# Another division of the PSUM banks at the end of the first FFN and in the second FFN

## The chip, the cores and the metric

The kernel runs on one core of one Trainium2 chip. The metric is device time in microseconds (us); the change is judged by its median over several runs. A profiled execution gives the trace: for each engine, what ran when and what it had waited for. Engines: PE (TensorE, matrix multiply; PEld is its weight load), DVE (VectorE), ACT (ScalarE), POOL (GpSimd), SP (which issues the DMAs). Matrix products land in PSUM, which this kernel divides into eight banks of 128 partitions by 512 fp32 values. Results leave a bank through DVE or ACT.

## The reference

Input `x` has 4 sequences of 1024 tokens with 128 features. Three layers with residuals follow one another:

```
x = x + 0.5 * ffn(layernorm(x))
x = x + attn(layernorm(x))          # which normalises once more, and adds its own input
x = x + 0.5 * ffn(layernorm(x))     # the same weights as the first

ffn:  weights = routing(x @ Wr)                 # 8 experts, dense: every expert is computed
      h_e = silu(x @ Wg[e]) * (x @ Wu[e])       # 128 -> 128
      out = sum_e weights[:, e] * (h_e @ Wd[e])
attn: 16 heads of 64, latents of 64 for queries and for keys and values, rotary positions,
      softmax(q k^T / 8) v, output projection
```

## The kernel before, in words

**Blocks.** Tokens are worked in 8 blocks of 512 (`blk`), each through 8 experts (`e`), so an FFN has 64 steps, `n = 8 blk + e`. Each engine works through its own instructions in the order in which the program lists them, which is written out by hand. An instruction that waits holds up those behind it on its engine.

**Banks.** `psA` is two banks (`ps_a` in the trace), `psS[0]` to `psS[3]` are one each (`ps_s`), then `psC` and `psX`. `aux()` (lines 101 to 104) hands out the banks of the list `self.rest` in turn; transposes and other small products use it. A new writer of a bank waits until the last reader of its former content is done; the trace shows this also for readers of other columns of the bank.

**First FFN** (`ffn`, line 364). A step multiplies gate and up (L400) into two of `psS[0..2]`, applies silu on ACT (L402) and the product on DVE (L408). Three steps later `down` (L365 to L372) multiplies by `Wd` into `psC` or `psX`; in the step after that, `gather` scales the result by the routing weights. In blocks 4, 6 and 7 ACT does that (L383, four instructions) and POOL adds it to `X` (L384). In the last 15 steps `self.rest` holds `psX` and `psS[3]` (L829), since the first attention work uses them, and all downs go to `psC`. The last three downs (experts 5, 6, 7 of block 7) have no other step of the FFN between them.

**Attention.** Scores (L703), exponentials (L707), sums on POOL (L719), values (L726), a pass that finds row maxima (L675, L676), and the making of rotated queries and keys for later heads in between (L593 to L615): products into two banks (L593), four products with tables on DVE (L581), a rounding on ACT (L607), a remainder on POOL (L612), and two DMAs out; the latents for it (C_l) are loaded by a DMA on SP (L586 through the helper at L47). Scores of odd slots use `psS[2]` and `psS[3]`.

**Second FFN** (`ffn2`, line 415). The gate and up products of a step (L479) take two of `psS[0]`, `psS[1]`, `psS[2]`, `psC`. ACT applies silu (L482), DVE multiplies twice (L492 with the up product, L493 with the routing weight), ACT rounds (L486), POOL forms the remainder (L487). Three steps later `down` (L434) adds three products to the sum of the block, over all 8 experts, in one bank: `psS[3]` for even blocks, `psX` for odd ones (L432). Four steps after the block's last step ACT copies the sum out (L447), one step later PE transposes it (L453) and DVE adds it to `X` (L455), which SP writes out. The last block does this in two halves.

Beside it, in the first steps, the last two attention outputs are projected (L771) and added (L773), and `ffn_pre` prepares blocks 6 and 7: norm (L227), transposes (L256), two copies on DVE (L258, L259), router logits (L269), read by DVE (L270), then the routing (L290 to L348) and a transpose of the weights (L357). All of these products take their bank from `aux()`, whose list holds one bank here, the first of `psA` (L960).

Of the kernel before, what the change touches and what calls it, by code (L numbers as in the profile page):

```python
# [17 lines left out]
B, S, D = 4, 1024, 128  # L18
H, DH = 16, 64
E = 8  # L20
# [17 lines left out]
class Kernel:  # L38
# [325 lines left out]
    def ffn(self, hp, tp, xs_of, wts, bg, depth, acts):  # L364
        nc, X = self.nc, self.X  # L365
        hs, gathers = [], []

        def down(blk, e, hT):
            pd = self.psX if e % 2 and self.psX not in self.rest else self.psC
            for i in range(4):  # L370
                nc.tensor.matmul(pd[:, i * 128:(i + 1) * 128], hT[:, i * 128:(i + 1) * 128], self.wd[:, e, :], start=True, stop=True)  # L371
            gathers.append((blk, e, pd))  # L372

        def gather(blk, e, pd):
            t = blk * 4
            assert blk in self.routed, (blk, e, len(self.routed))
            if e % 4 == 0 and blk not in acts:
                for i in range(4):
                    nc.vector.scalar_tensor_tensor(X[:, t + i, :], pd[:, i * 128:(i + 1) * 128], wts[:, t + i, e:e + 1], X[:, t + i, :], ALU.mult, ALU.add)
            else:  # L380
                tmp = tp.tile([128, 4, 128], F32, name="dtmp", tag=f"t{e % 3}")
                for i in range(4):
                    nc.scalar.activation(tmp[:, i, :], pd[:, i * 128:(i + 1) * 128], AF.Identity, scale=wts[:, t + i, e:e + 1])  # L383
                nc.gpsimd.tensor_tensor(X[:, t:t + 4, :], X[:, t:t + 4, :], tmp, ALU.add)  # L384
            if e == E - 1:
                self.done.add(blk)

        for n in range(2 * B * E + depth + 1):
            if gathers:
                gather(*gathers.pop(0))  # L390
            sh = None
            if n < 2 * B * E:
                blk, e = divmod(n, E)
                xs = xs_of(blk)
                assert blk in self.ready
                bg(n, 0)
                ps = [self.psS[(2 * n + k) % 3] for k in range(2)]
                for w, p in zip((self.wg, self.wu), ps):
                    for k, (a, c) in enumerate(((0, 0), (0, 1), (1, 0))):
                        nc.tensor.matmul(p, w[:, a, e, :], xs[:, c, :], start=k == 0, stop=k == 2)  # L400
                sh = hp.tile([128, 2, 512], F32, name="p")
                nc.scalar.activation(sh[:, 0, :], ps[0], AF.Silu)  # L402
                bg(n, 1)
            if len(hs) == depth or (hs and sh is None):
                down(*hs.pop(0))
            if sh is not None:
                bg(n, 2)
                nc.vector.tensor_tensor(sh[:, 1, :], sh[:, 0, :], ps[1], ALU.mult)  # L408
                bg(n, 3)
                hs.append((blk, e, sh[:, 1, :]))  # L410
        for g in gathers:
            gather(*g)


    def ffn2(self, xs_of, bg, out):
        nc, X = self.nc, self.X
        N, DEPTH, LEAD, NB = 2 * B * E, 3, 4, 4
        nbank = 0
        hs, later, wbs, split = [], {}, [], []

        def weights(n):
            blk, e = divmod(n, E)
            assert blk in self.routed, blk
            wb = self.prep.tile([128, 512], F32, name="wb", tag=("t0", "t1", "t2", "t3", "hi_r")[n % 5])
            h = blk % 2
            nc.sync.dma_start(out=wb, in_=self.wt_scr[blk // 2][e:e + 1, 512 * h:512 * h + 512].to_broadcast([128, 512]))
            wbs.append(wb)

        def down(n, sh):
            blk, e = divmod(n, E)  # L430
            if e == 0:
                self.po = (self.psS[3], self.psX)[blk % 2]  # L432
            for k, (a, c) in enumerate(((0, 0), (1, 0), (0, 1))):
                nc.tensor.matmul(self.po, self.wd[:, a, e, :], sh[:, c].bitcast(F32R), start=e == 0 and k == 0, stop=e == E - 1 and k == 2)  # L434
            if e == E - 1:
                finish(n, blk, self.po)

        def finish(n, blk, po):
            o = self.prep.tile([128, 512], F32, name="fo", tag="xs2")
            last = blk == NT // 4 - 1  # L440
            t = blk * 4
            parts = [slice(0, 2), slice(2, 4)] if last else [slice(0, 4)]

            def copy():
                for p in parts:
                    c = slice(128 * p.start, 128 * p.stop)
                    nc.scalar.copy(o[:, c], po[:, c])  # L447

            def turn():
                for p in parts:  # L450
                    pt = self.aux()
                    for i in range(p.start, p.stop):
                        nc.tensor.transpose(pt[:, i * 128:(i + 1) * 128], o[:, i * 128:(i + 1) * 128], self.ident)  # L453
                    xs = X[:, t + p.start:t + p.stop, :]
                    nc.vector.tensor_tensor(xs, xs, pt.rearrange("p (t d) -> p t d", t=4)[:, p], ALU.add)  # L455
                    nc.sync.dma_start(out=out[:, t + p.start:t + p.stop, :], in_=xs)

            for k, fn in enumerate((copy, turn)):
                if last:
                    fn()  # L460
                else:
                    later.setdefault(n + DEPTH + 1 + k, []).append(fn)

        for n in range(LEAD):
            weights(n)
        for n in range(N + DEPTH):
            for fn in later.pop(n, ()):
                fn()
            if n < N:
                blk, e = divmod(n, E)  # L470
                xs = xs_of(blk)
                assert blk in self.ready
                ps = []
                for _ in range(2):
                    ps.append(self.psS[nbank % NB] if nbank % NB < 3 else self.psC)
                    nbank += 1
                for w, p in zip((self.wg, self.wu), ps):
                    for k, (a, c) in enumerate(((0, 0), (0, 1), (1, 0))):
                        nc.tensor.matmul(p, w[:, a, e, :], xs[:, c, :], start=k == 0, stop=k == 2)  # L479
                gh = self.op1.tile([128, 2, 512], F32, name="ptmp") if n % 3 == 2 else self.prep.tile([128, 2, 512], F32, name="eo", bufs=2)  # L480
                g, h = gh[:, 0, :], gh[:, 1, :]
                nc.scalar.activation(g, ps[0], AF.Silu)  # L482
            if split:
                m, hp = split.pop()
                sh = self.pp.tile([128, 2, 512], F32R, name="p")
                nc.scalar.copy(sh[:, 0, :], hp)  # L486
                (nc.gpsimd if m < N - 1 else nc.vector).tensor_tensor(sh[:, 1, :], hp, self.f(sh[:, 0, :]), ALU.subtract)  # L487
                hs.append((m, sh))
            if hs and hs[0][0] == n - DEPTH:
                down(*hs.pop(0))  # L490
            if n < N:
                nc.vector.tensor_tensor(h, g, ps[1], ALU.mult)  # L492
                nc.vector.tensor_tensor(h, h, wbs.pop(0), ALU.mult)  # L493
                split.append((n, h))
                if n + LEAD < N:
                    weights(n + LEAD)
                bg(n)
# [279 lines left out]
    def run(self):  # L777
# [88 lines left out]
        a, c, e = (NP - 3) % 3, (NP - 2) % 3, (NP - 1) % 3  # L866
# [90 lines left out]
        with ExitStack() as ctx:  # L957
            self.ready, self.routed = set(range(6)), set(range(6))
            assert not (streams[1] or streams[2])
            self.rest, self.bankO = [self.psA[:, 0, :]], None  # L960
            last = [self.accp.tile([128, 2, 512], F32R, name="acc") for _ in range(2)]
            x_of = lambda blk: last[blk - 6] if blk >= 6 else xs[blk // 2][:, :, 512 * (blk % 2):512 * (blk % 2) + 512]
            g = self.ffn_pre(self.prep, (6, 7), x_of, self.wts2[:, 3].rearrange("p e t -> p t e"), rows=3)

            def bg2(n):
                self.run_later(NGRP + 1 + n)
                if n >= GS:
                    next(g, 0)
                if n >= GD:
                    next(g, 0)  # L970

            self.ffn2(x_of, bg2, self.out.rearrange("(n p) d -> p n d", p=128))
# [55 lines left out]
```

## Time and profile before

| | us |
|---|---|
| median of 3 runs | 1803.73 (1801.5 to 1804.94) |
| the profiled execution's own time | 1803.11 |
| its span, first to last instruction | 1801.3 |
| PE busy | 1726.3 (96%) |
| DVE busy | 1339.9 (74%) |
| POOL busy | 1339.3 (74%) |
| ACT busy | 908.9 (50%) |
| 234.5 to 242.4: PE busy, of 7.9 | 5.24 |
| 1699.0 to 1706.0: PE busy, of 7.0 | 1.80 |
| 1637 to 1802: all waits of PE | 13.0 |

The shares of the page are means over the whole span; what a wait is worth depends on the stage. The first FFN ends and attention begins near 242, and the second FFN runs from 1637.6 to the end. PE is shown with the clock that it was granted, 1.00 being full speed; the mean over the span is 0.989. In a timeline line the first number is the start, the second the duration, then come engine, line, operation, output <- inputs and a count; brackets hold the idle time before it and what ended it. A down projection of four matmuls shows as x8, since each runs as two passes.

### The profile page before, as it was taken

What the parts mean: (1) busy time and instruction counts of PE and PEld (TensorE: products, weight loads), DVE (VectorE), ACT (ScalarE), POOL (GpSimd) and SP (SyncE); (2) the same over time, 40 slices, a digit from 0 to 9 for tenths busy, and PEclk for the clock granted to TensorE, in tenths of its full rate; (3) what the DMA queues carried; (4) which work ended last, traced back from release to release, by engine and by line L of the source; (5) the groups of instructions that cost most, each with busy time, mean ns of one, the idle gap of its engine ahead of it and who ended that gap; (6) DMA issues with size and microseconds to landing.
All of it is one profiled execution on the core that took longest, in us unless ns stands there. A gap on an engine that the chain in (4) does not pass through costs nothing.

```text
span 1801.3 us, 31304 instructions
## 1 busy us (share of the span) xinstructions
PE 1726.3 (96%) x11492; PEld 1030.3 (57%) x11492; DVE 1339.9 (74%) x1903; ACT 908.9 (50%) x1916; POOL 1339.3 (74%) x803
## 2 busy tenths in 40 slices
PE   7988889999999999999999999999999999999898
PEld 5777655555555555555555555555555555556676
DVE  6776658877777778777688777788777776835787
ACT  4666555444545445554444445454444444445454
POOL 4458678778887788877788777788888765556566
PEclk9999989999999999999999999999999999999899
DMA  6025445444444444454444544454444432124443
GB/s 196 1 71 170 135 129 165 145 145 147 130 142 142 150 145 130 130 153 142 141 135 136 160 140 131 143 142 147 136 144 140 130 95 72 31 96 129 129 124 100
DMA packets 129674, 232.80 MB, mean 129 GB/s; under 512 B 36336, under 2 KB 49776, under 8 KB 128880
## 3 DMA queue, kind: packets, MB, share of 16 engines
q1 hardware_dynamic: 129520, 230.80, 42.7%
q8 instruction: 90, 1.47, 0.4%
q14 instruction: 64, 0.52, 0.1%
HBM read 146.45 MB, written 84.02 MB: 128 GB/s over the span
## 4 chain that ended last, share of the span: by engine, by line
PE 78%; DVE 7%; ACT 7%; POOL 3%; issue 3%; DMA 1%; SPq 1%; ACTq 0%; POOLq 0%; DVEq 0%
PE psc L726 24%; PE ps_s L703 21%; PE ps_a L675 8%; PE ps_s L738 5%; ACT p L707 4%; PE psx L771 4%; PE ps_s L400 3%; PE ps_s L479 3%; PE psx L593 2%; DVE m L676 2%; PE psc L371 1%; PE psc L479 1%; PE psx L434 1%; PE ps_s L434 1%; ACT dtmp L383 1%
## 5 line engine op out<-in xcount | busy, mean ns | idle before, releaser
L676 DVE TENSOR_REDUCE m<-ps_a 128x2 f32<-128x1024 f32 x512 | 627.3, 1225 | 324.1 <-PE ps_a L675 323.9
L707 ACT ACTIVATE p<-ps_s 128x512 f32<-128x512 f32 x1024 | 531.0, 601 | 605.6 <-PE ps_s L703 605.4
L719 POOL TENSOR_TENSOR acc<-acc,p 128x1024 f32<-128x1024 f32 x256 | 609.7, 2382 | 43.0 <-ACT p L707 31.6
L726 PE MATMUL psc<-p,ckn 128*64 128x512 f32 x2048 | 496.2, 605 | 0.0
L703 PE MATMUL ps_s<-QT,KT 64*128 64x512 f32 x3072 | 447.3, 393 | 0.1
L719 POOL TENSOR_TENSOR acc<-p 128x1024 f32<-128x1024 f32 x64 | 152.2, 2377 | 251.4 <-ACT p L707 251.3
L703 PEld LDWEIGHTS ps_s<-QT,KT 64*128 64x128 f32 x3072 | 296.7, 185 | 60.2 <-issue 3.2
L726 PEld LDWEIGHTS psc<-p,ckn 128*64 128x64 f32 x2048 | 124.3, 136 | 213.7 <-issue 199.4
L675 PE MATMUL ps_a<-KT,QT 64*128 64x512 f32 x1024 | 234.6, 450 | 11.2 <-DVE m L676 11.0
L675 PEld LDWEIGHTS ps_a<-KT,QT 64*128 64x128 f32 x1024 | 98.5, 184 | 229.9 <-issue 83.8
L703 PE MATMUL ps_s<-maxr,one_row 64*128 64x512 f32 x1024 | 210.0, 392 | 1.0 <-DMA maxr<-mr 1.0
L612 POOL TENSOR_TENSOR eo<-eo,hi_r 128x512 fp32r<-128x512 f32 x128 | 185.0, 1463 | 0.0
L766 DVE TENSOR_TENSOR osb<-osb,rB 128x512 f32<-128x512 f32 x64 | 153.8, 2403 | 3.0 <-DMA rB<-d 3.0
L384 POOL TENSOR_TENSOR X<-X,dtmp 128x512 f32<-128x512 f32 x54 | 69.0, 1278 | 73.2 <-ACT dtmp L383 66.7
L703 PEld LDWEIGHTS ps_s<-maxr,one_row 64*128 64x128 f32 x1024 | 103.4, 185 | 23.0 <-DMA maxr<-mr 2.2
L487 POOL TENSOR_TENSOR p<-eo,p 128x512 fp32r<-128x512 f32 x42 | 62.6, 1496 | 42.0 <-ACT p L486 35.5
L602 POOL TENSOR_TENSOR eo<-rt,rt 128x512 f32<-128x512 f32 x64 | 81.8, 1279 | 0.0
L600 POOL TENSOR_TENSOR eo<-rt,rt 128x512 f32<-128x512 f32 x64 | 81.8, 1278 | 0.0
L607 ACT CAST hi_r<-eo 128x512 fp32r<-128x512 f32 x128 | 74.6, 640 | 6.9 <-DMA qs<-hi_r 3.6
L400 PE MATMUL ps_s<-xs,wg 128*128 128x512 f32 x192 | 66.6, 457 | 11.8 <-DVE p L408 10.7
L728 ACT COPY osb<-psc 128x512 f32<-128x512 f32 x64 | 37.6, 588 | 72.8 <-PE psc L726 72.8
L771 PEld LDWEIGHTS psx<-G,osb 128*128 128x128 f32 x496 | 60.8, 193 | 21.2 <-issue 21.2
(194 smaller groups left out, 2131.8 us busy)
## 6 DMA issues: line engine op xcount, KB each, us to landing
C_l<-cs SPq DMA_DIRECT2D x64, 512.0 KB
QT<-qs SPq DMA_DIRECT2D x256, 128.0 KB
KT<-ks SPq DMA_DIRECT2D x256, 128.0 KB
qs<-hi_r SPq DMA_DIRECT2D x32, 512.0 KB
qs<-eo SPq DMA_DIRECT2D x32, 512.0 KB
ks<-hi_r SPq DMA_DIRECT2D x32, 512.0 KB
ks<-eo SPq DMA_DIRECT2D x32, 512.0 KB
rB<-d SPq DMA_DIRECT2D x128, 128.0 KB
```

Source lines behind the costliest of these rows:

```text
L400: nc.tensor.matmul(p, w[:, a, e, :], xs[:, c, :], start=k == 0, stop=k == 2)
L600: nc.gpsimd.tensor_tensor(w["eo"][:, 0, :], w[0, 0], w[1, 1], ALU.subtract)
L612: nc.gpsimd.tensor_tensor(eo.bitcast(F32R), eo, self.f(w["hi"][:, int(stage[2]), :]), ALU.subtract)
L675: nc.tensor.matmul(self.psA[:, hh, :], self.QT[P % 3][r, 0, q0:q0 + 128], self.KT[P % 3][r, 0, kk * 512:kk * 512 + 512], start=True, stop= ...
L676: nc.vector.tensor_reduce(self.m_of[U][:, :, qb, kk], self.psA, AX.X, ALU.max)
L703: nc.tensor.matmul(ps, w, x, start=k == 0, stop=k == 3)
L707: nc.scalar.activation(self.p_of[s][:, hh, :], ps, AF.Exp, scale=0.125)
L719: nc.gpsimd.tensor_tensor(acc, self.p_of[s - 1] if c == 1 else acc, self.p_of[s], ALU.add)
L726: nc.tensor.matmul(self.psC[64 * hh:64 * hh + 64, :], self.ckn[b % 2][:, c, :], self.p_of[s][:, hh, :], start=c == 0, stop=c == 7)
L738: nc.tensor.matmul(pd[32 * n:32 * n + 32, 0:256], self.ones, part[:, n // 2, 256 * (n % 2):256 * (n % 2) + 256], start=k == 0, stop=k == D ...
L766: nc.vector.tensor_tensor(osb, osb, rB, ALU.mult)
L771: nc.tensor.matmul(po[:, i * 128:(i + 1) * 128], osb[:, i * 128:(i + 1) * 128], self.G[:, j, :], start=True, stop=True)
```

## The change

Three edits. The downs of experts 6 and 7 of the last block of the first FFN go to `psX` and `psS[3]`. The sums of the second FFN all go to `psX`. The list of `aux()` during the second FFN gets `psS[3]` as its second bank, so that the products that use it alternate between two banks. No instruction is added to the work or taken from it, and the order on each engine stays as it was.

```diff
         def down(blk, e, hT):
             pd = self.psX if e % 2 and self.psX not in self.rest else self.psC
+            if blk == 2 * B - 1 and e >= E - 2:
+                pd = (self.psX, self.psS[3])[e % 2]
             for i in range(4):
...
         def down(n, sh):
             blk, e = divmod(n, E)
             if e == 0:
-                self.po = (self.psS[3], self.psX)[blk % 2]
+                self.po = self.psX
...
-            self.rest, self.bankO = [self.psA[:, 0, :]], None
+            self.rest, self.bankO = [self.psA[:, 0, :], self.psS[3]], None
```

## The prediction

> **What bounds the kernel now.** I read the page's shares first (TensorE, PE, is busy 96% of the span; the chain that ended last is 78% PE), then asked for the waits of PE over the two stages that the change touches, and then their timelines. Where PE is the bound, a PE wait counts one for one unless another engine is as late. The attention stage between them (some 250 to 1637 us) is not edited; it can only start earlier.
>
> First place, the end of the first FFN. Columns: start, duration, engine, line, what it does, count, and in brackets the idle time before it and who ended it.
>
> ```profile
> 234.58 1.16 PE L371 MATMUL psc<-wd,p 128*128 128x128 f32 x8 [2.26 <-ACT dtmp L383]
> 235.84 1.14 ACT L383 ACTIVATE dtmp<-psc,wts 128x128 f32<-128x128 f32 x4 [1.31 <-PE psc L371]
> 237.03 2.07 PE L371 MATMUL psc<-wd,p 128*128 128x128 f32 x8 [1.29 <-ACT dtmp L383]
> ...
> 239.20 1.14 ACT L383 ACTIVATE dtmp<-psc,wts 128x128 f32<-128x128 f32 x4 [2.22 <-PE psc L371]
> 240.40 2.07 PE L371 MATMUL psc<-wd,p 128*128 128x128 f32 x8 [1.29 <-ACT dtmp L383]
> ...
> 242.57 1.14 ACT L383 ACTIVATE dtmp<-psc,wts 128x128 f32<-128x128 f32 x4 [2.22 <-PE psc L371]
> ...
> 243.85 1.27 POOL L384 TENSOR_TENSOR X<-X,dtmp 128x512 f32<-128x512 f32 x1 [2.10 <-ACT dtmp L383]
> ...
> 245.09 2.51 POOL L612 TENSOR_TENSOR eo<-eo,hi_r 128x512 fp32r<-128x512 f32 x2
> ...
> 248.05 0.46 SPq L47 DMA_DIRECT2D C_l<-cs  x1
> ```
>
> Three down projections (experts 5, 6, 7 of the last block) share one bank, so PE and ACT take turns. The last addition on POOL follows, then POOL's L612, and behind it on the SP queue the load of C_l, for which PE waits at 252.39 (1.69 us idle). That chain is the bound here, not PE.
>
> Second place, the second FFN:
>
> ```profile
> 1699.95 1.65 ACT L227 ACTIVATE yf<-X,rstdf 128x128 f32<-128x128 f32 x4 [2.18 <-DVE rstdf L222]
> ...
> 1702.49 0.58 ACT L447 COPY fo<-ps_s 128x512 f32<-128x512 f32 x1
> ...
> 1704.40 0.21 DVE L270 TENSOR_REDUCE z<-ps_a 128x32 f32<-128x64 f32 x1
> ...
> 1704.76 1.08 PE L256 MATMUL ps_a<-ident,yf 128*128 128x128 f32 x4 [5.20 <-DVE z L270]
> ...
> 1705.49 1.63 PE L479 MATMUL ps_s<-QT,QT 128*128 128x512 f32 x3
> ```
>
> The transposes of block 7 (L256) have their input at 1701.60 but share a bank with the router logits of block 6, which DVE reads at 1704.40. Of 13.0 us that PE waits from 1637 to 1802, this one is 5.2. From 1740 to 1790 PE is busy 50.00 of 50.00 us.
>
> **Part 1, banks for the last downs.** Only experts 6 and 7 of block 7 move; expert 5 still starts at 234.58, since it waits for ACT after the exponential table load. A down at full clock takes 1.05 us (the row at 230.84), so 6 and 7 end at 236.8 and 237.85. Neither bank is in use: DVE's last reads of them end by 221.9. ACT then runs its three groups of 1.14 back to back, 235.84 to 239.26 instead of 243.71. POOL's three additions of 1.27 end at 240.85 instead of 245.12; its 2.51 us of L612 end at 243.36; the C_l load is issued 0.45 later and, with the 4.3 us from issue to use that it takes now, lets PE go at 248.1: **4.3 us** earlier. The transfers ahead of it (loads of the next head pair, 256 GB/s until 242.4) are over by then, so it meets the same empty queue. PE gets there even earlier: 4.5 us from the gaps and 1.6 from two score groups (1.71 us each at half clock now, 242.57 to 244.28; 0.93 at full, 248.21). It just waits 3.5 us instead of 1.69. Step 1's scores use the bank of expert 7; they are due at 239.2, and ACT has freed it at 239.26: nothing to pay.
>
> What can cut this is the granted clock. It fell to half at 236.05 and came back near 246.3, in steps of 3.41 us:
>
> ```profile
> 232.64:236.05 3.41, 1.16 (x8) 0.97 (x8) 1.54 (x2) 2.09 (x7) 2.04 (x2) 1.00 0.92 250
> ...
> 249.69:253.10 3.41, 1.72 (x16) 0.99 (x12) 2.25 (x9) 1.96 (x4) 2.71 (x2) 1.00 0.60 179
> ```
>
> The columns are stretch, length, busy us of PE, its weight loads, DVE, ACT, POOL, then the clock. A stretch with 1.16 us of PE work was followed by half clock, one with 1.72 was not. After the change the first holds 1.47 (234.58 to 236.05), between the two. The Trainium skill (TensorE: Matmul & The Clock Gate, on HAM oscillation) puts it as a rule: no PE gap above about 3.4 us. By the rule this place, with gaps of 2.26 us, keeps full clock and gains 4.3; but the row shows the clock falling with no gap that long, so I don't trust it. If it falls, 6 and 7 end at 237.6 and 239.65, ACT at 240.8, POOL's L612 at 244.6 instead of 247.60: 3.0. The longer wait for C_l may cool PE after it; at most 1.7 us (half of 3.41), of which a wait of 0.81 at 255.36 hides half. Ends 2.0 and 4.3; since 1.47 lies in the middle I take **3.6**.
>
> **Part 2, two banks for transposes.** The two transposes and the logits alternate, so L256 waits only for its inputs: it ends at 1701.9 instead of 1705.84, and the next score groups start then. PE also loses what the clock cost it after the stall (half clock 1700.4 to 1710.6; 1.63 and 1.48 us for groups that take 0.85). Following PE group by group (1.37 for two score groups, 0.7 a down, 0.6 for L453, 0.95 for L269) it is 5.1 us earlier at the scores now at 1713.33. But DVE is next: z still ends at 1704.61, then 0.69 + 0.69 for L258 and L259, L492 and L493 (0.69 + 1.0), L455 0.68, L492 and L493 again (0.69 + 1.6), z 0.21: its multiply now at 1715.08 starts at 1711.0, **4.1** earlier. The routing that follows holds PE twice for DVE (1.19 at 1728.40, 1.45 at 1739.51), so DVE's gain is what lasts. Ends: 5.1 if DVE finds air in its 1.89 us of idleness before L317; 2.5 if the clock still falls (1.7 less for PE) and DVE's L493 is the slow form twice. I take **4.0**.
>
> At the very end the two halves no longer share a bank. Now the second waits 0.60 for DVE's read of other columns of the same bank. With its own bank DVE's last addition runs right behind the one that ends at 1797.27 instead of at 1798.11: **0.8** (0.4 if the output DMA hides half). Other steps only change bank at equal cost.
>
> **Part 3, one bank for sums.** Here a rule speaks against the change. The skill (PSUM — Partial Sum Buffer, on bank collisions) says to guard by bank, so the first down of a block must wait for ACT's copy of the block before. Taken alone that costs a copy, 0.58 us, at each of seven boundaries: 4.1 us. The rows show a score pair of 1.4 us between last and first down. Copy end against the next weight load: 1662.47/1662.85, 1679.51/1679.86, 1703.07/about 1703.3 as reckoned, 1748.08/1748.43, 1765.37/1765.30, 1782.03/1782.17: five free, one 0.07 late. The seventh is not:
>
> ```profile
> 1728.97 0.66 PEld L434 LDWEIGHTS ps_s<-p,QT 128*128 128x128 f32 x3
> 1729.10 0.62 ACT L486 CAST p<-eo 128x512 fp32r<-128x512 f32 x1 [2.52 <-DVE eo L493]
> ...
> 1729.63 0.58 ACT L447 COPY fo<-psx 128x512 f32<-128x512 f32 x1
> ```
>
> The copy is queued behind L486, which waits for DVE, and ends 1.24 after the down started. L453, queued behind that down, waits for the same copy until 1730.26 anyway; scores slip 0.75, and the two DVE waits of 0.38 and 1.45 that follow swallow it. So **-0.2** in all; ends 0 and -1.5 (the 1.24 not swallowed, plus small ones).
>
> **Sum.** 3.6 + 4.0 + 0.8 - 0.2 = 8.2 us. The profiled execution took 1803.11 (span 1801.3 and 1.8 around it), 0.6 under the median of the runs; 1794.9 from the one, 1795.5 from the other. I say **1795.2**. A change of 0.2%, 3.6 us, is about what a measurement of this kernel can tell from none.
>
> **Rivals.** (a) The first gain is hidden: C_l lands no sooner because transfers, not POOL, set it. Against: the DMA share is 0.00 to 0.04 from 243 to 248. Time 1803.1 - 4.6 = 1798.5. (b) DVE is the bound of the whole second FFN (57.3 of 65.7 us from 1730, waits on both sides), so that stall returns as DVE waits. Against: DVE is idle 2.25 and 1.27 us around the stall. Time 1803.1 - 3.6 - 0.6 = 1798.9. (c) Both: 1802.5, no change. (d) Slower: the single sum bank. With PE earlier and DVE not, the copy sits behind a late L486 at every boundary as it does at 1729.63. It must reach (8.4 + 3.6)/7 = 1.7 us a boundary to be slower; at 2.0, time 1803.1 - 8.4 + 14 = 1808.7. The ACT idleness of 2.52 speaks for it, the five free boundaries against it.
>
> **How the numbers follow.** Forecast 0.72, (a) 0.08, (b) 0.10, (c) 0.05, (d) 0.05. The forecast's own bounds are 10.2 (4.3 + 5.1 + 0.8) and 3.4 (2.0 + 2.5 + 0.4 - 1.5): 1793 to 1799.7. The range 1791.5 to 1800.2 adds a little scatter and holds (a) and (b). Faster: nearly all of the first and about two thirds of (a) and (b), 0.83; same 0.12; slower 0.05.
>
> **What would show it.** Downs of experts 6 and 7 right behind 5; L593's first start near 248; no DVE wait before the second L256 and its scores near 1702 less the shift; the last addition right behind its neighbour; PE waits on L447 below 0.3 us but for one boundary. It would be wrong if L593 doesn't move, if waits for L492 grow by what the stall gives, or if L434 begins to wait for L447 at most boundaries.

## The result, and the profile after

| | before | changed |
|---|---|---|
| median of the runs timed together, us | 1804.54 (1801.5 to 1805.81) | 1798.32 (1795.41 to 1800.34) |
| the profiled execution's own time | 1803.11 | 1798.04 |
| mean granted clock of PE | 0.989 | 0.991 |
| start of the first of the last downs (expert 5) | 234.58 | 235.86 |
| from there to the first product with C_l | 17.81 | 14.21 |
| from there to the first denominators of attention, the sums of its exponentials (L740, was L738) | 32.53 | 30.49 |
| from those to the first gate product of the second FFN | 1370.53 | 1372.00 |
| from that product to the end of the span | 163.64 | 157.83 |

The changed kernel takes 0.9964 of the time before (0.9951 to 0.9977), which is 6.5 us less by that ratio: faster, as forecast. The two profiled executions differ by 5.10 us of span, and the last four rows account for them, each stretch beginning where the one above it ends: -2.04 at the end of the first FFN, +1.47 in the attention stage, -5.81 in the second FFN, and +1.28 (row four) before the first changed instruction. The two positive terms stand in code that was not edited.

Lines behind the edit have moved by two: L371 is now L373, L593 is L595, L447 is L449 (by more where an experiment adds lines of its own). First the timeline of the changed kernel where the first FFN ends (start, duration, engine, line, what, count, idle time before it and who ended that):

```profile
235.86 1.16 PE L373 MATMUL psc<-wd,p 128*128 128x128 f32 x8 [2.25 <-ACT dtmp L385]
...
236.85 1.61 PE L373 MATMUL psx<-wd,p 128*128 128x128 f32 x8
...
238.25 1.91 PE L373 MATMUL ps_s<-wd,p 128*128 128x128 f32 x8
...
240.27 1.14 ACT L385 ACTIVATE dtmp<-ps_s,wts 128x128 f32<-128x128 f32 x4 [0.56 <-PE ps_s L373]
...
241.55 1.29 POOL L386 TENSOR_TENSOR X<-X,dtmp 128x512 f32<-128x512 f32 x1 [0.43 <-ACT dtmp L385]
...
242.80 2.50 POOL L614 TENSOR_TENSOR eo<-eo,hi_r 128x512 fp32r<-128x512 f32 x2
...
245.75 0.46 SPq L47 DMA_DIRECT2D C_l<-cs  x1
...
250.07 0.50 PE L595 MATMUL psx<-C_l,wup 64*128 64x512 f32 x1 [3.22 <-DMA C_l<-cs]
...
251.33 3.37 PE L728 MATMUL psc<-p,ckn 128*64 128x512 f32 x8
```

The three downs now name three banks and follow one another; the two waits of 1.29 us for ACT are gone. The second and third last longer than the first because the clock has halved. POOL's last addition, its L614, the C_l load and L595 follow in the same chain as before. The wait for C_l at the end of it has grown from 1.69 to 3.22 us, and the values product behind it takes 3.37 us where the kernel before took 1.94:

```profile
252.39 0.49 PE L593 MATMUL psx<-C_l,wup 64*128 64x512 f32 x1 [1.69 <-DMA C_l<-cs]
...
253.49 1.94 PE L726 MATMUL psc<-p,ckn 128*64 128x512 f32 x8
```

The stretches of the changed kernel's trace (from:to, length; busy us of PE, PEld, DVE, ACT and POOL with their counts; granted clock, DMA share, GB/s) say why:

```profile
233.80:237.20 3.40, 1.34 (x12) 1.34 (x13) 1.66 (x2) 2.08 (x7) 2.08 (x2) 1.00 0.76 222
237.20:240.60 3.40, 3.40 (x17) 3.17 (x17) 0.00 (x0) 2.53 (x10) 2.04 (x3) 0.50 0.98 236
...
247.40:250.80 3.40, 0.73 (x6) 0.49 (x6) 1.39 (x2) 0.39 (x1) 3.24 (x3) 1.00 0.56 178
250.80:254.20 3.40, 3.40 (x11) 0.85 (x9) 1.48 (x3) 0.00 (x0) 1.70 (x1) 0.50 0.00 1
```

Twice a stretch in which PE had little to do is followed by one at half clock: once at the downs, as before (there it lasted 10.24 us, here 3.41), and once behind the wait for C_l, where the profile of before has full clock.

The second FFN, timeline:

```profile
1700.70 1.65 ACT L227 ACTIVATE yf<-X,rstdf 128x128 f32<-128x128 f32 x4 [2.18 <-DVE rstdf L222]
1701.25 1.63 PE L256 MATMUL ps_s<-ident,yf 128*128 128x128 f32 x4 [1.05 <-ACT yf L227]
...
1702.53 1.63 PE L481 MATMUL ps_s<-QT,QT 128*128 128x512 f32 x3
...
1705.16 0.21 DVE L270 TENSOR_REDUCE z<-ps_a 128x32 f32<-128x64 f32 x1
...
1710.87 0.69 DVE L494 TENSOR_TENSOR ptmp<-ptmp,psc 128x512 f32<-128x512 f32 x1 [0.16 <-PE psc L481]
...
1726.07 0.96 PE L436 MATMUL psx<-p,QT 128*128 128x512 f32 x3 [0.89 <-ACT fo L449]
```

L256 writes `ps_s` and starts with its input, 3.9 us ahead of DVE's read of the logits, which it used to wait for. The gate and up products behind it start at 1702.53 instead of 1705.49. The last line is the price of the single sum bank: one down that waits 0.89 us for ACT's copy. DVE's multiply that the prediction followed starts at 1710.87; before, it was this line:

```profile
1715.08 0.69 DVE L492 TENSOR_TENSOR ptmp<-ptmp,psc 128x512 f32<-128x512 f32 x1 [0.53 <-ACT ptmp L482]
```

### The profile page after: what moved, and what is told of

The parts are those of the page before. It is cut to its first block, busy times and chain, and to the rows that moved or that the text cites. A ratio compares the mean times of both kernels' runs of the same rounds, so it can differ in the third digit from the quotient of the medians.

```text
span 1796.2 us, 31299 instructions
## 1 busy us (share of the span) xinstructions
PE 1724.6 (96%) x11492; PEld 1027.7 (57%) x11492; DVE 1340.3 (75%) x1903; ACT 908.9 (51%) x1916; POOL 1339.0 (75%) x803
## 3 DMA queue, kind: packets, MB, share of 16 engines
q8 instruction: 90, 1.47, 0.3%
## 4 chain that ended last, share of the span: by engine, by line
PE 79%; DVE 7%; ACT 6%; POOL 3%; issue 2%; DMA 2%; SPq 1%; DVEq 0%; ACTq 0%; POOLq 0%
PE psc L728 25%; PE ps_s L705 21%; PE ps_a L677 8%; PE ps_s L740 5%; ACT p L709 4%; PE psx L773 4%; PE ps_s L402 3%; PE ps_s L481 3%; PE psx L595 2%; PE psx L436 2%; DVE m L678 2%; PE psc L373 1%; PE psc L481 1%; PE ps_s L687 1%; POOL acc L721 1%
## 5 line engine op out<-in xcount | busy, mean ns | idle before, releaser
L614 POOL TENSOR_TENSOR eo<-eo,hi_r 128x512 fp32r<-128x512 f32 x128 | 184.9, 1463 | 0.0
```

The source lines that it names most:

```text
L614: nc.gpsimd.tensor_tensor(eo.bitcast(F32R), eo, self.f(w["hi"][:, int(stage[2]), :]), ALU.subtract)
```

## The experiments

Each result is a ratio to the kernel before, with a 95% interval from runs on one chip; what is called so many us less is reckoned from the ratio. A figure with a plus sign is counted from the start of expert 5's down, and is read from one profiled execution. The first four ran beside one another (before: 1803.88), the last four beside one another (before: 1805.87).

**The first edit alone**, with the banks of the second FFN left as they were:

```diff
+            if blk == 2 * B - 1 and e >= E - 2:
+                pd = (self.psX, self.psS[3])[e % 2]
```

> Only the first edit: experts 6 and 7 of the last block of the first FFN in banks of their own; the second FFN as before. Theory: the chain ACT, POOL, load of C_l is shortened by 3.6 us, and a half-clock stretch behind the longer wait for C_l gives back about 1.6 of it, so the time falls by 2.0 us (1801.7 to 1803.0 with 1804.5 before; ratio near 0.9989). In the profile L593's first start comes 3 to 4.3 us sooner after the down of expert 5 than the 17.81 us of before, and a clock of 0.50 shows behind it. Rival, the gain is kept whole: 3.6 us or more, ratio 0.9980 or less. Rival, nothing is left of it when attention is under way: ratio 1.000, and the first denominators (L738) no sooner after the down of expert 5 than in before (32.53 us).

1802.4 us, 0.9989 (0.9981 to 0.9997): 2.0 us less. Its timeline has the same end of the chain:

```profile
249.70 0.60 PE L595 MATMUL psx<-C_l,wup 64*128 64x512 f32 x1 [3.60 <-DMA C_l<-cs]
```

L595 starts 14.62 us after the first of the last downs instead of 17.81, so the chain is 3.2 us shorter; but the first denominators are only 1.66 us sooner (30.87 for 32.53). Half the gain is lost between these two places, with nothing of the second FFN changed.

**The two edits of the second FFN alone:**

```diff
-                self.po = (self.psS[3], self.psX)[blk % 2]
+                self.po = self.psX
...
-            self.rest, self.bankO = [self.psA[:, 0, :]], None
+            self.rest, self.bankO = [self.psA[:, 0, :], self.psS[3]], None
```

> Only the two edits of the second FFN: one bank for its sums, two for its transposes; the first FFN as before. Theory: the second FFN, 163.66 us from its first gate product to the end in the profile of before, takes 157 to 159, so the time falls by 4.6 to 5.9 us (ratio 0.9967 to 0.9975). Rival, the change's whole gain lies here and the first edit brings nothing: ratio equal to that of the whole change, 0.9964 or less. Rival, DVE is the bound there: less than 2 us, ratio above 0.9989.

1798.39 us, 0.9970 (0.9958 to 0.9982): 5.4 us less. The second FFN took 159.42 us, 4.2 less than before. It fell a little short of the 157 to 159 expected; in this execution the half clock at its stall lasted 6.83 us, in the changed kernel 3.41. Its first FFN, which is that of before, shows something else: L593 comes at +17.75, as before, but half clock falls behind its wait for C_l too (1.76 us), and the denominators come at +34.03 instead of +32.53. The product of the two ratios, 0.9959, is what the whole change should give.

**The single sum bank alone:**

```diff
-                self.po = (self.psS[3], self.psX)[blk % 2]
+                self.po = self.psX
```

> Only the sums of the second FFN in one bank, with the one bank for transposes as before. Theory: six of the seven boundaries have the copy done before the first down of the next block needs the bank, and the slip at the seventh is swallowed by DVE waits: 0 to 0.5 us slower than before, ratio 1.0000 to 1.0003. Rival, the rule of the bank taken alone: a copy of 0.58 us at each of seven boundaries, 4.1 us, ratio 1.0023; PE then waits for L447 at each boundary. Rival, the seventh boundary is paid in full: 1.2 us, ratio 1.0007.

1803.6 us, 0.9999 (0.9989 to 1.0009): nothing. The waits of PE in its second FFN (the waiter, whom it waited for; total us, times, longest):

```profile
PE ps_a L256 <- DVE z L270: 5.2, 1, 5.2
...
PE psx L434 <- ACT fo L447: 0.9, 1, 0.9
```

The stall of 5.2 us stays, since the transposes still have one bank. One boundary of seven waits, for 0.9 us. L479's wait for DVE shrinks from 2.6 to 2.2, L453's for the copy from 0.7 to 0.5. The estimate of a copy at each boundary, 4.1 us, is not what happens. In this execution the half clock at the stall lasted 6.83 us instead of the 10.24 of before, and DVE's multiply behind it came 1.2 us sooner with the stall itself unchanged.

**The change, with the C_l load issued early.** In the kernel before, SP issues that load behind stores that wait for POOL's remainders; here it goes ahead of them, before the attention work starts:

```diff
         self.load(1)
+        self.rope(NROPE, "fetch")
...
-        rope(-1, {-2: "fetch"})
```

> The whole change, and the first load of C_l of the attention stage is listed on SP right behind the loads of the next head pair, ahead of the two stores that wait for POOL. Theory: POOL's remainder and the store behind it set when C_l comes; with the load ahead of them PE no longer waits at L595 (3.22 us in the profile of the change) and doesn't fall to half clock behind it, so L595 starts 11 to 12 us after the down of expert 5 instead of 14.21, and the time falls by 2 to 4.5 us against the change (ratio to before 0.994 to 0.9955). Rival, the transfers set it: C_l comes no sooner since 2 MB are ahead of it, no gain. Rival, POOL is the bound behind it: L595 starts sooner, but the first denominators (L740, 30.49 us after the down of expert 5 in the change) come less than 1 us sooner.

1793.97 us, 0.9948 (0.9936 to 0.9960). Timeline:

```profile
240.81 0.42 SPq L47 DMA_DIRECT2D C_l<-cs  x1
...
245.84 0.49 PE L595 MATMUL psx<-C_l,wup 64*128 64x512 f32 x1 [0.25 <-DMA C_l<-cs]
...
246.94 1.94 PE L728 MATMUL psc<-p,ckn 128*64 128x512 f32 x8
```

Counted from the first of the last downs (235.75 here), the load is issued at +5.06 instead of +9.89, and L595, at +10.09 (11 to 12 were expected), waits 0.25 us. The values product takes 1.94 us, and the denominators come at +25.39, 5.1 sooner than the change brings them. In this execution the clock did not fall at the downs either.

**The change, with PE kept busy in the wait for C_l.** Three products into a bank that L595 overwrites, their results unused:

```diff
+            if n == NROPE:
+                for _ in range(3):
+                    nc.tensor.matmul(ps[0], self.ident, self.cos[:, 0:512], start=True, stop=True)
```

> The whole change, and three matrix products whose result nobody reads, ahead of the first product with C_l (L595) of the attention stage, into the bank that this product overwrites: PE is busy for about 2.7 of the 3.2 us in which it waits for C_l. Theory: L595 still starts about 14.2 us after the down of expert 5, since POOL and the load set it, but no half-clock stretch follows near 250, the values (L728 of the change, 3.37 us there) take 1.9 to 2.0 again, and the first denominators (L740 of the change) come 28.5 to 29.2 us after the down of expert 5 instead of 30.49. The time falls by 1.3 to 1.8 us against the change. Rival, the slow values are not the clock's doing but wait on something else: 30.4 us as before, although the clock stays at 1.00. Rival, the products run past the landing of C_l: L595 starts later than 14.5.

1794.17 us, 0.9941 (0.9928 to 0.9954). Timeline:

```profile
246.26 2.84 PE L594 MATMUL psx<-cos,ident 128*128 128x512 f32 x6
...
249.47 0.49 PE L598 MATMUL psx<-C_l,wup 64*128 64x512 f32 x1 [0.37 <-DMA C_l<-cs]
...
250.56 1.94 PE L731 MATMUL psc<-p,ckn 128*64 128x512 f32 x8
```

C_l comes no sooner (+14.14 to L598, the L595 of the change at +14.21), yet the values product is back to 1.94 us and the denominators are at +28.86, 1.6 sooner than in the changed kernel. So what takes back nearly half of the first gain is the clock, and not the wait itself.

**The change, with PE kept busy ahead of the last downs.** Two unused products before expert 5's down:

```diff
+            if n == 2 * B * E:
+                for _ in range(2): nc.tensor.matmul(self.psX, self.ident, self.cos[:, 0:512], start=True, stop=True)
```

> The whole change, and two matrix products whose result nobody reads, ahead of the down of expert 5, in the 2.25 us in which PE waits for ACT's table load there. Theory: the clock does not fall behind it, the downs of experts 6 and 7 take 1.05 us instead of 1.61 and 1.91, and L595 starts 13.5 us after the down of expert 5 instead of 14.21 (17.81 less the 4.3 of the prediction's full-clock case). Rival, the fall of the clock doesn't hang on how busy PE was in the 3.4 us before: half clock again near 237 and 14.2. The time itself moves by less than 1 us, which is under the scatter.

1796.39 us, 0.9951 (0.9937 to 0.9966). Timeline:

```profile
236.56 1.06 PE L373 MATMUL psx<-wd,p 128*128 128x128 f32 x8
237.46 1.06 PE L373 MATMUL ps_s<-wd,p 128*128 128x128 f32 x8
...
249.47 0.79 PE L598 MATMUL psx<-C_l,wup 64*128 64x512 f32 x1 [4.08 <-DMA C_l<-cs]
...
251.36 3.68 PE L731 MATMUL psc<-p,ckn 128*64 128x512 f32 x8
```

The downs run at full clock, 1.06 us each, but L598 comes only 0.3 us sooner (+13.91, where 13.5 was expected) and PE waits 4.08 us instead of 3.22 for it. Half clock then lasts 6.83 us, and the denominators are at +31.38, 0.9 us *later* than in the changed kernel. With the downs at full clock the next wait is longer, and half clock follows that one.

**The change once more,** to see its scatter in the second set:

> The changed kernel once more. Theory: the second half-clock stretch inside attention (near 1077 in the profile of the change; that of before has one, near 1420) depends on where the stretches of 3.41 us happen to fall and not on the change: attention from the first denominators to the second FFN takes 1370 to 1371 us with one such stretch and 1372 to 1372.5 with two, whichever the kernel. From the first and the second edit alone, 2.0 and 5.4 us, the change should gain 7.4 us in a larger sample, ratio 0.9959, against the 0.9964 measured. Rival, the change costs attention something: 1372 with two stretches every time, and 0.9964 or more again.

1796.57 us, 0.9958 (0.9944 to 0.9973), close to the product of the two halves. In this execution the clock stayed up at the downs without any filling; L595 came at +13.75 after a wait of 3.92 us, the half clock behind it lasted 6.83 us, and the denominators came at +30.86: much what the filled downs gave. Both clock cases of the prediction exist, in one and the same kernel.

**Everything at once:** the early load, the two products before the downs, and one unused product before block 7's first transpose in the second FFN, so that the clock stays up there too:

```diff
+            if rows == 3 and h: nc.tensor.matmul(ps, self.ident, self.cos[:, 0:512], start=True, stop=True)
```

> The whole change, the first load of C_l ahead of the stores that wait for POOL, the two products ahead of the down of expert 5, and one such product ahead of the transposes of block 7 in the second FFN (while PE waits there for ACT's norm). Theory: against the version with the early load alone (ratio to before 0.9948) 0.7 us from the downs at full clock and 0.5 to 1.0 us from the second FFN if the half-clock stretch near 1701 stays away: 157.9 us of the second FFN become 156.9 to 157.4, ratio 0.9940 to 0.9945. Rival, DVE holds that stage and the clock there is worth nothing: 157.9 again; or the extra product delays the transposes: above 158.2.

1794.88 us, 0.9942 (0.9930 to 0.9954). One stretch behind the former stall:

```profile
1701.00:1704.00 3.00, 3.00 (x19) 2.62 (x18) 2.96 (x5) 1.23 (x3) 1.30 (x1) 1.00 0.40 120
```

The clock is full and PE has no gap, but DVE is busy 2.96 of 3.00 us. The second FFN takes 157.78 us, and 157.83 in the changed kernel, where 3.41 us ran at half clock; 156.9 to 157.4 were expected. DVE sets what follows the stall, and making up those 3.41 us of half clock adds nothing (6.83 us did cost 1.3 there, in the kernel with the second FFN's edits alone). The gain expected from the downs did not show either: the denominators come at +25.71, where the early load alone, with its downs at full clock by chance, gave +25.39.

The early load (0.9948), the filled wait (0.9941) and all together (0.9942) lie under the changed kernel's two samples (0.9964 and 0.9958), by 2 to 4 us. Their intervals touch those of the changed kernel, so of these gains only what the traces show at the place itself is established, and they can't be ranked among themselves. The early load is the plainest of them, since it adds no product and leaves no wait to fill.

## Why the prediction was right, point by point

**The whole.** 1795.2 was forecast, 1798.32 and 1796.57 were measured, inside the range and on the forecast side. The time alone would not have told the forecast from its rivals: 1798.32 lies next to the 1798.5 of (a) and the 1798.9 of (b), and only the traces and the single edits decide. The predicted sum was 8.2 us. What the edits gained where they act is 2.04 + 5.81 = 7.85; the profiled execution shows 5.10, because of the two terms outside the edited code, and the ratio over all runs 6.5. Part of the 7.85 is itself the clock of these two executions, as parts 2 and the end show.

**Part 1: mechanism right, gain nearly twice what was measured.** The chain is the one described: downs back to back, ACT's groups, POOL's additions and L614, the load, L595. It is 3.60 us shorter (17.81 to 14.21), the very 3.6 that was taken. That is luck in part: the clock did fall, a case worked out at 3.0, but the two downs then ended 0.4 and 0.8 us sooner than reckoned. With full clock it was 3.90 and 4.06 (the filled downs and the second execution) where 4.3 was worked out; POOL's three additions took 4.01 us there, and not 3.81.

The mis-sized term is the sentence "The longer wait for C_l may cool PE after it; at most 1.7 us (...), of which a wait of 0.81 at 255.36 hides half". It was named, and it stands in the lower end, 2.0, but not in the 3.6. It measured 1.56 us in the changed kernel (3.60 at L595, 2.04 at the denominators) and 2.39 in its second execution (4.06 and 1.67, with 6.83 us of half clock). The filled wait settles that this is the clock: same arrival, 1.94 instead of 3.37 us for the values, 1.6 us regained. The loss is no property of the change alone: the old first FFN lost 1.5 us in the same way in one of its three profiled executions (+34.03, against +32.53 and +32.57). The first edit alone is worth 2.0 us by its ratio, the low end of the prediction.

The clock at the downs was left between two cases, and rightly: it fell at 237.2 after 1.34 busy us, and stayed up in the second execution. The rule of the Trainium skill (TensorE: Matmul & The Clock Gate, HAM oscillation), no gap above some 3.4 us, was rightly not trusted: the longest gap before that fall was 2.25 us. What the prediction did not see is that the case hardly matters: sooner downs meet a longer, colder wait, as the filled downs and the second execution show.

**Part 2: right, and 0.9 us too small in this execution.** From the second FFN's first gate product, the scores of the eighth step of block 6 come at 70.78 instead of 75.69 and DVE's multiply behind them at 72.52 instead of 77.44: 4.9 us, where DVE was reckoned to allow 4.1 and PE 5.1. The mis-sized term is L492 and L493 (now L494 and L495), taken with 1.0 and 1.6 us for the second of each pair; they took 0.69 and 1.33, which is 0.6 of the 0.9. The reading that DVE, not PE, holds what is gained is shown by the kernel with everything at once.

The size hangs on the clock as well: the lead kept to the last step is 4.8 to 5.0 us in the executions of the changed banks with half clock of 3.41 us or none at the stall, and 3.5 where it lasted 6.83 (the second FFN's edits alone). The old stall varied too: 10.24 us of half clock in the profile of before, 6.83 with the first edit alone (0.2 us sooner than before) and with the sum bank alone (1.2 sooner). With 6.83 us on both sides the second transpose bank thus brings 2.3 to 3.3 us, and the rest of the 4.9 goes with the shorter half clock. That the change shortens it is likely, since the stall with one transpose bank had at least 6.83 us in three executions and that with two had less in six of seven; no run separates it.

**The end.** From the start of ACT's last copies to DVE's last addition took 2.41 us and now takes 1.24, before and after:

```profile
1795.70 0.65 ACT L447 COPY fo<-psx 128x256 f32<-128x256 f32 x2 [1.32 <-PE psx L434]
...
1798.11 0.42 DVE L455 TENSOR_TENSOR X<-X,ps_a 128x256 f32<-128x256 f32 x1 [0.84 <-PE ps_a L453]
...
1791.57 0.65 ACT L449 COPY fo<-psx 128x256 f32<-128x256 f32 x2 [1.32 <-PE psx L436]
...
1792.47 0.42 DVE L457 TENSOR_TENSOR X<-X,ps_s 128x256 f32<-128x256 f32 x1 [1.50 <-PE ps_s L455]
1792.81 0.41 DVE L457 TENSOR_TENSOR X<-X,ps_a 128x256 f32<-128x256 f32 x1
```

The two additions read two banks and stand back to back. What follows the last grew by 0.2 us, so 0.97 is left, against 0.8 predicted.

Half of it is the clock, at which the prediction did not look here: before, it fell to half at 1795.9, ahead of the last transposes; in the changed kernel it was full until 1793.7, behind them. The kernel with the first edit alone has the old single bank and full clock at this place: 5.08 us from the copies to the end of the span, against 5.58 before and 4.60 in the changed kernel. So the bank brings 0.5 us at full clock, and 0.7 at half (4.85 in the kernel with the second FFN's edits alone).

**Part 3: right.** One boundary of seven waits, the one named, for 0.89 us. The lead over the kernel before, both counted from the first gate product, is 4.92 us at DVE's multiply ahead of it, 4.17 behind it at the scores of step 36 (block 4, expert 4), and 4.86 again at step 40: the slip of 0.75 and the later waits that swallow it are both there. Alone, the single bank costs nothing that can be measured (0.9989 to 1.0009).

**The rivals.** (a) falls: C_l landed sooner, and 4.32 us from issue to use is the same as the 4.3 before. (b) and (c) fall as forecasts of no gain: DVE is the bound of the second FFN, but only after it gave 4.9 us at the stall, and PE's waits for its multiply (L492, now L494) did not grow: 3.6 us in all before, 3.1 after. (d) falls by the changed kernel itself, with PE earlier and still one wait of 0.9 us for ACT's copy, and by the sum bank alone.

**Open.** The attention stage, unedited, took 1369.6 to 1370.7 us in the profiled executions with no or one half-clock stretch in it, and 1372.0 to 1372.4 in those with two, whichever the kernel. The 1.47 us lost there goes together with that. That the change causes the second stretch is not shown: the changed kernel had two in both its executions, and so had each half of it alone, but with C_l loaded early there was one, and with PE kept busy ahead of L595 or of the downs none. No experiment took up the place where they fall (near 1077 and 1421 us). The 1.28 us before the first edited instruction is the scatter of that lead-in, which ran from 234.58 to 239.98 over the ten executions.

## What to carry to other kernels

When a wait of PE is removed, follow the chain to the next wait: here it grew from 1.69 to 3.22 us, and half clock behind it took back 1.6 of 3.6 us. A load that depends on nothing should be issued ahead of stores that wait for another engine; at the first denominators, moving one DMA brought 5.1 us on top of the banks of the last downs, which brought 2.0. Of the kernel's time 1.8 to 2.9 us of that show, by the ratios, and those are not clear of the scatter. In a stage whose second engine is nearly full, price a removed stall by that engine's own rows: it gave 4.9 us at the stall, and the stage was only 0.05 us shorter still when PE's clock was mended as well.

## What the runs showed of the hardware that was not expected

The granted clock changes on a grid of about 3.41 us: half clock lasted 3.41, 6.83 or 10.24 us at all the places above but the end of the span. Whether a stretch falls goes with how busy PE was in the one before, and no gap as long as a stretch is needed: before the fall at 237.2 the longest was 2.25 us. In the ten traces together, from 30 us on, each of the 50 full-clock stretches of that length with less than 1.47 us of PE was followed by half clock, and none with more than 2.3. Of the 105 in between 24 were: 1.65 us fell in the kernel with the second FFN's edits alone (at 254.4), and 1.98 in the kernel before (at 1700.4), while 1.72 stayed up there (249.69, shown in the prediction). What decides in that band is open.

One stretch cost 1.4 us at a values product of 1.94 (3.37), so a wait of PE can have a second price behind it. It depends on where the stretches lie over the work: at the same downs of the same program the stretch held 1.34 us of PE in one execution and fell, and 1.86 in the next and did not.
